# A two-layer graph attention kernel: attention products between two sets of scores, first loads from one queue, and rearranged closing steps

## The chip, the cores and the metric

The kernel runs on one core of a Trainium2 chip. A core has five engines with their own instruction streams: TensorE (PE in the profile) multiplies matrices, VectorE (DVE) and ScalarE (ACT) work element by element, GpSimd (POOL) does too, and SyncE (SP) issues most of the data transfers (DMAs). They wait for each other by semaphores. The metric is the time on the device in microseconds for one execution; the time of a kernel is the median of its runs.

## The reference, cut to what matters

The input is `x`, 128 sequences of 128 rows with 512 features, and `adj`, a mask of 128x128 for each sequence. Two layers follow each other, each with a residual and a layer norm, everything in float32:

```
x = layernorm(x + gnn0(x, adj))     # 4 heads of 64: softmax(where(adj, q k^T / 8, -max)) v, then @ Wo + bo
x = layernorm(x + gnn1(x, adj))     # norm(x)*gamma+beta, 8 heads of 64, mask adj | eye, then @ w_out^T + b_out
```

`gnn0` projects with Wq, Wk, Wv (512 to 256 each) and Wo (256 to 512); `gnn1` has one projection `w_qkv` (512 to 3 x 512) and `w_out` (512 to 512).

## The kernel before, in words

Sequences are handled in 64 groups of two (`G = 2`). The projections are done with a scheme of seven products in place of eight (Strassen's): the two sequences of a group and the two halves of the features are the blocks, `sums` and `weight_sums...` make the added operands, and product numbers 1 to 7 accumulate into the banks `a`, `c` and `f` of PSUM (`INTO`). `product_0` does it for layer 0's projection, `qk` and `v` (through `product`) for layer 1's, `out_product` for both output projections.

The order of the work on every engine is written out by hand (`manual_schedule`): each engine executes in the order in which the program calls it. The main part is `step(s)` for s = 2 to 63, a software pipeline over groups. In step s TensorE does

* the scores of group s - 1 in layer 0 (part 0: both sequences, four heads each) and of group s - 4 in layer 1 (part 1: its first sequence, eight heads; part 2: its second), in `scores`;
* the products of probabilities and values, in `attend`, for group s - 2 in layer 0 (part 0) and s - 5 in layer 1 (parts 1 and 2);
* layer 0's projection of group s, layer 0's output projection of group s - 2, layer 1's projections of group s - 3 and its output projection of group s - 5.

Scores take 64 rows of the array per matmul, two heads side by side; attention products take 64 columns; all the others take the whole array. Between scores and attention products, VectorE puts the scores through the mask into an SBUF tile that POOL has filled with the low value (`masked`, `cleared`), takes row maxima (`maxima`); ScalarE does the exponentials (`exps`); POOL divides by the totals (`normalised`); VectorE turns blocks of 32x32 (`blocks`), and the probabilities are written to DRAM by SyncE and fetched transposed (`put` and `fetch` in `probs_arrive`). Keys and queries of layer 1 take the same kind of way (`kq_arrive`), and ScalarE makes `qo` of them (`q_in_order`, L430). In the first groups and the last ones TensorE transposes instead.

`opening` handles groups 0 and 1 and prepares the weights: `load_transposed` fetches rows of `w_qkv` and `w_out` into buffers that are not in use yet, and `prepare` turns them on TensorE. `closing_a`, `closing_b` (twice) and `last` empty the pipeline: fewer kinds of matmuls are left there to fill the time in which softmax passes through the other engines. `flush` runs norms that were put off; the last group's norm is in `norm_plain`.

PSUM has eight banks: four tiles that rotate (`mm_tile`) and four with fixed names, `a`, `f`, `a0`, `f0`. Layer 1's `v` products use `a` and `f`, as do the attention products of parts 0 and 1; the scores of part 1 use `a0` and `f0`. After products 1, 5 and 6 ScalarE copies the bank (a "tap", L375 and L489) before the next product is accumulated onto it.

In `step`, the stretch around the first part of the change reads:

```python
        made = scores(s)
        ...
        masked(made, s, 0, 1, 2)
        if s == 3:
            turn(s - 3)
            arrive(s - 3)
        attend(s)
        maxima(s, 0, 1)
        out_sums(0, s - 2)
```

Of the kernel before, what the change touches and what calls it, by code (L numbers as in the profile page):

```python
# [17 lines left out]
P = 128  # L18
# [9 lines left out]
def kernel(ctx: ExitStack, tc: tile.TileContext, x, adj, wq, wk, wv, wo, bo,  # L28
# [64 lines left out]
    def load(g):  # L93
        load_rows(g)
        load_mask(g)
# [26 lines left out]


# [3 lines left out]
    nc.vector.tensor_copy(eye, ident)  # L127
# [3 lines left out]

    HF = INNER[0] // 2
    w0 = const.tile([P, KC, 3, 2, HF], F32, name="w0")
    ws0 = const.tile([P, 3, KC // 2, 3, HF], F32, name="ws0")
    for i, w in enumerate((wq, wk, wv)):
        for a in range(4):
            (nc.sync if i else nc.scalar).dma_start(
                w0[32 * a:32 * a + 32, :, i].rearrange("p c h f -> p c (h f)"),
                w[a * P:(a + 1) * P].rearrange("(c i) f -> i c f", i=32))
    load_mask(0)  # L140
    load_rows(0)
    load(1)
    wo0 = const.tile([P, INNER[0] // P, E], F32, name="wo0")
    nc.sync.dma_start(wo0, wo.rearrange("(c p) f -> p c f", p=P))
    bias0 = const.tile([P, E], F32, name="bias0")
    nc.sync.dma_start(bias0, bo[None, :].to_broadcast([P, E]))
    bias1 = const.tile([P, E], F32, name="bias1")
    nc.sync.dma_start(bias1, b_out[None, :].to_broadcast([P, E]))

    transposed(0)  # L150
    load_quarters(1)
# [3 lines left out]
    gb_raw = one.tile([2 * KC, P], F32, tag="sm2", name="gb_raw")  # L155
    gb = const.tile([P, 2 * KC], F32, name="gb")

    setup = []
    def load_transposed(dst, src, name):
        rows, cols = src.shape  # L160
        raws = []
        for r in range(rows // P):
            raw = spare.pop(0)
            nc.sync.dma_start(raw, src[r * P:(r + 1) * P, :])
            raws.append(raw)

        def part(r):
            raw = raws[r]
            pt = mm_tile(f"{name}t_{r}")
            for c in range(cols // P):  # L170
                nc.tensor.transpose(pt[:, c * P:(c + 1) * P], raw[:, c * P:(c + 1) * P], ident)
            to = dst[:, :, r * P:(r + 1) * P]
            pt = pt.rearrange("p (c f) -> p c f", f=P)
            if r % 2:
                nc.scalar.copy(to, pt)
            else:
                nc.vector.tensor_copy(to, pt)

        setup.extend(lambda r=r: part(r) for r in range(rows // P))

    nc.sync.dma_start(gb_raw[:KC], gamma.rearrange("(c p) -> c p", p=P))
# [7 lines left out]


# [23 lines left out]
    def weight_sums_0():  # L214
        combine(*(w0[:, c:c + KH, :, h] for c in (0, KH) for h in range(2)), *(ws0[:, i] for i in range(3)))
# [8 lines left out]

    load_transposed(w1, w_qkv, "w_qkv")
    setup.append(turn_gamma_beta)
    load_transposed(wo1, w_out, "w_out")

    setup.append(setup.pop(-3))
# [71 lines left out]
    def finish_direct(g):  # L301

        xT = XT[1, g] = one.tile([P, KC, T], F32, tag="xT1", name=f"xT1_{g}")
        for b in range(G):
            pt = mm_tile(f"ht{g}_{b}")
            for c in range(KC):
                nc.tensor.transpose(pt[:, c * N:(c + 1) * N], R[g][:, b, c * P:(c + 1) * P], ident)
            for c in range(KC):
                o, i = xT[:, c, b * N:(b + 1) * N], pt[:, c * N:(c + 1) * N]
                scale, bias = gb[:, c:c + 1], gb[:, KC + c:KC + c + 1]  # L310
                if b == 0:
                    nc.scalar.activation(o, i, AF.Identity, bias=bias, scale=scale)
                else:
                    nc.vector.tensor_scalar(o, i, scale, bias, op0=ALU.mult, op1=ALU.add)
        sums(1, g)
# [21 lines left out]
    def product(kind, g, i, take=True):  # L337
# [15 lines left out]
        if first and which == "c":  # L353
            ACC[kind, which] = mm_tile(f"{kind}{which}_{g}")
        elif first:
            ACC[kind, which] = ps_st.tile([P, 512], F32, tag=which, name=f"{kind}{which}_{g}")
# [94 lines left out]
    def product_0(g, *which):  # L451
# [6 lines left out]
        for i in which:  # L458
# [4 lines left out]
            bank, first = INTO[i]  # L463
            if first and bank == "c":
                ACC[0, bank] = mm_tile(f"c0_{g}")
            elif first:
                ACC[0, bank] = ps_st.tile([P, 512], F32, tag=f"{bank}0", name=f"{bank}0_{g}")
            acc = ACC[0, bank]
            parts = acc[:, :3 * P].rearrange("p (t n) -> p t n", n=P)
            if g in PLAIN_0:  # L470
                todo = [(parts[:, (t + odd) % 3], *((right[:, c, t], left[:, c]) if t < 2 else
                                                    (left[:, c], right[:, c, t])))
                        for t in range(3) for c in range(KH)]
# [5 lines left out]
            for n, (o, lhsT, rhs) in enumerate(todo):  # L479
                nc.tensor.matmul(o, lhsT, rhs, start=first and n == 0, stop=n == len(todo) - 1,  # L480
                                 skip_group_check=True)
            src = acc[:, :3 * P]
# [290 lines left out]
    def norm_plain(g, b):  # L773
        row = R[g][:, b]
        n = E // 2
        acc = ACC["op", b]
        st = two.tile([P, 2, nc.vector.BN_STATS_DIM], F32, tag="st_last", name=f"st_last{b}")
        for i in range(2):
            h = slice(i * n, (i + 1) * n)
            nc.vector.tensor_add(row[:, h], acc[:, h], row[:, h])  # L780
            nc.vector.bn_stats(st[:, i], row[:, h])
        mv = two.tile([P, nc.vector.BN_AGGR_DIM], F32, tag="mv", name=f"mv_last{b}")
        nc.vector.bn_aggr(mv, st)
        ve, root = (two.tile([P, 1], F32, tag=t, name=f"{t}_last{b}") for t in ("ve1", "root1"))
        nc.gpsimd.tensor_scalar(ve, mv[:, 1:2], 1.0, EPS, op0=ALU.mult, op1=ALU.add)
        nc.gpsimd.tensor_tensor(root, ve, mhalf[:, :1], op=ALU.pow)
        nc.vector.tensor_scalar(row, row, mv[:, 0:1], root, op0=ALU.subtract, op1=ALU.mult)
        nc.sync.dma_start(out[g * G + b], row)


# [13 lines left out]
    def opening():  # L804
# [4 lines left out]
        for h in range(2):  # L809
            nc.scalar.activation(w0[:, :, 0, h, :], w0[:, :, 0, h, :], AF.Copy, scale=SCALE)  # L810
        product_0(0, 1)
        weight_sums_0()
        product_0(0, 2, 5, 6, 3)
# [31 lines left out]
    def step(s):  # L845

        made = scores(s)
# [6 lines left out]
        masked(made, s, 0, 1, 2)  # L854
        if s == 3:
            turn(s - 3)
            arrive(s - 3)
        attend(s)
        maxima(s, 0, 1)
# [8 lines left out]
        maxima(s, 2)  # L868
# [57 lines left out]
        if s in (3, 4):  # L926
            second = product("v", s - 3, 2, take=False)
            v(s - 3, 1)
            second()
        else:  # L930
            v(s - 3, 1, 2)
# [21 lines left out]
    def closing_a():  # L953
# [31 lines left out]
        blocks(s, 1)  # L985
        exps(s, 2, 1)
# [6 lines left out]
        exps(s, 0, 0)  # L993
        blocks(s, 2)
        probs_arrive(s, 1, 2)
# [8 lines left out]
        cleared(s + 1, 1, 2)  # L1004
# [6 lines left out]
    def closing_b(s):  # L1011

        made = scores(s, 1, 2)
        masked(made, s, 1, 2)
        v(s - 4, 1, 2)
        maxima(s, 1)
        v(s - 4, 6, 5)
        exps(s, 1, 0)
        flush()
        v(s - 4, 7, 3)  # L1020
        maxima(s, 2)
        v(s - 4, 4)
        exps(s, 1, 1)
        normalised(s, 1)
        attend(s, 1, 2)
        out_sums(1, s - 5)
        blocks(s, 1)
        finish_direct(s - 3)
        out_product(1, s - 5, 1, 2)
# [3 lines left out]
        out_product(1, s - 5, 5, 6)  # L1033
        qk(s - 3, 1)
        exps(s, 2, 1)
        out_product(1, s - 5, 7, 3)
        qk(s - 3, 2)
        normalised(s, 2)
        out_product(1, s - 5, 4)
        qk(s - 3, 6)  # L1040
        blocks(s, 2)
        probs_arrive(s, 1, 2)
# [6 lines left out]
        out_product(0, s - 2, 7)  # L1049
        qk(s - 3, 3)  # L1050
        out_product(0, s - 2, 4)
        cleared(s + 1, 1, 2)
# [9 lines left out]
    def last():  # L1062
# [36 lines left out]
        norm_plain(NG - 1, 0)  # L1099
        norm_plain(NG - 1, 1)  # L1100
# [37 lines left out]
```

## Time and profile before

| what | us |
|---|---|
| median of 3 runs | 2755.77 (2754.71 to 2757.05) |
| profiled execution, its own time | 2756.88 |
| span of the profiled execution | 2755.1 |
| TensorE busy | 2725.6 |
| VectorE, POOL, ScalarE busy | 2026.3, 1753.5, 1505.7 |

The profile is of one execution. The span runs from the first instruction to the last; the execution's own time contains 1.8 us more around it. In the lists that follow, a line such as `1312.53 1.16 PE L551 MATMUL sc<-rawqk,qkv ... x16` gives the start in us from the span's start, the length in us, the engine, the line of the kernel, the operation, the tile written and the tiles read, their shapes, and how many records were merged. A float32 matmul leaves two records. A wait is given as who waited, for whom, the sum, how often, and the longest. Matmuls overlap and their ends are modelled, so lengths of work on TensorE are best taken from start to start.

### The profile page before, as it was taken

Reading aid. Unit: us, or ns where it says so; the run is one execution under the profiler, and the core shown is the slowest. Engines: PE = TensorE matmul, PEld = TensorE weight load, DVE = VectorE, ACT = ScalarE, POOL = GpSimd, SP = SyncE. Lnnn points to the kernel's source line nnn. Section 1 sums busy time; section 2 is a strip of 40 time slices with the busy share of each in tenths; the row PEclk is TensorE's granted clock in tenths of the full one; section 3 lists DMA queues with packets and bytes.
Section 4 is the critical chain, followed back from the end, with each engine's and each line's share of the span. In section 5 each row is a group of like instructions: output and inputs, shape, how many; then the busy total and the mean of one; then the engine's idle time right before and its main releaser. Section 6 shows DMA issues by size and latency. Waiting matters only on the chain.

```text
span 2755.1 us, 49293 instructions
## 1 busy us (share of the span) xinstructions
PE 2725.6 (99%) x15781; PEld 2027.5 (74%) x15781; DVE 2026.3 (74%) x3662; ACT 1505.7 (55%) x4805; POOL 1753.5 (64%) x2311
## 2 busy tenths in 40 slices
PE   8999999999999999999999999999999999999998
PEld 7867777677776677776777766777767777667787
DVE  5777777777777777777777777777777777777664
ACT  3455565564564654655645546556556455465554
POOL 4566666666666666666666666666676666666664
PEclk9999999999999999999999999999999999999999
DMA  6567777777777777777777777777777777777741
GB/s 171 154 202 202 222 209 218 210 214 215 215 205 218 218 207 220 212 215 213 211 215 217 202 220 218 204 222 210 214 215 211 220 214 202 220 218 205 212 118 62
DMA packets 548561, 562.72 MB, mean 204 GB/s; under 512 B 55368, under 2 KB 465488, under 8 KB 548304
## 3 DMA queue, kind: packets, MB, share of 16 engines
q1 hardware_dynamic: 547728, 559.05, 71.6%
q8 instruction: 127, 2.08, 0.3%
q14 instruction: 130, 1.06, 0.1%
q10 hardware_dynamic: 576, 0.52, 0.1%
HBM read 300.95 MB, written 258.47 MB: 203 GB/s over the span
## 4 chain that ended last, share of the span: by engine, by line
PE 95%; DMA 2%; POOL 1%; ACT 1%; DVE 1%; issue 0%; SPq 0%; ACTq 0%; POOLq 0%; DVEq 0%
PE qka L365 16%; PE a L480 12%; PE oa L518 11%; PE qkf L365 8%; PE va L365 8%; PE av L680 6%; PE f L480 6%; PE of L518 6%; PE qkc L365 4%; PE vf L365 4%; PE c L480 3%; PE oc L518 3%; PE sc L551 2%; PE sc L557 2%; PE vc L365 2%; PE sc_a L557 2%
## 5 line engine op out<-in xcount | busy, mean ns | idle before, releaser
L601 ACT ACTIVATE sm<-sm,nmax 128x128 f32<-128x128 f32 x1536 | 595.2, 393 | 7.6 <-DVE nmax L592 6.0
L610 POOL TENSOR_TENSOR sm<-sm,rec 128x1024 f32<-128x1024 f32 x192 | 364.3, 1897 | 360.0 <-DVE rec L609 357.9
L702 POOL TENSOR_TENSOR r<-r,bias 128x1024 f32<-128x1024 f32 x128 | 301.7, 2358 | 126.7 <-ACT r L701 126.7
L522 DVE TENSOR_TENSOR r<-oa,r 128x256 f32<-128x256 f32 x508 | 212.0, 417 | 166.3 <-PE oa L518 131.4
L601 ACT ACTIVATION_READ_ACCUMULATOR sm<-sm,nmax 128x1 f32 x1536 | 295.2, 192 | 0.0
L375 ACT COPY ev<-va 128x256 f32<-128x256 f32 x128 | 47.7, 373 | 438.2 <-PE va L365 438.1
L628 DVE STREAM_TRANSPOSE turnedp<-sm 128x1024 f32<-128x1024 f32 x188 | 233.5, 1242 | 65.7 <-POOL sm L610 62.9
L721 POOL TENSOR_SCALAR ve<-mv 128x2 f32<-128x2 f32 x191 | 41.7, 218 | 371.7 <-DVE mv L714 361.1
L747 ACT ACTIVATE r<-r,shift,root 128x512 f32<-128x512 f32 x254 | 192.8, 808 | 85.8 <-POOL shift L736 85.8
L592 DVE TENSOR_REDUCE nmax<-sm 128x8 f32<-128x1024 f32 x192 | 226.1, 1203 | 0.1
L365 PE MATMUL qka<-wsqk,xs 128*128 128x512 f32 x472 | 221.8, 592 | 0.0
L365 PE MATMUL qkf<-w,xs 128*128 128x512 f32 x472 | 221.8, 592 | 0.0
L518 PE MATMUL oa<-wso,so 128*128 128x256 f32 x760 | 206.1, 380 | 2.3 <-POOL so L329 1.8
L518 PE MATMUL of<-wo,so 128*128 128x256 f32 x760 | 206.0, 380 | 0.7 <-POOL so L329 0.4
L329 POOL TENSOR_TENSOR xs<-xT 128x256 f32<-128x256 f32 x256 | 188.6, 737 | 26.8 <-DVE xT L118 23.2
L430 ACT ACTIVATE qo<-kq 128x512 f32<-128x512 f32 x118 | 67.9, 622 | 228.2 <-DMA kq<-scrkq 228.2
L480 PE MATMUL f<-w,xs 128*128 128x128 f32 (+1 forms) x760 | 182.1, 376 | 0.0
L480 PE MATMUL a<-ws,xs 128*128 128x128 f32 (+1 forms) x760 | 182.1, 375 | 0.0
L586 DVE COPY_PREDICATED sm<-m,sc 128x512 f32<-128x512 uint8 x256 | 172.3, 725 | 11.1 <-PE sc L551 2.2
L713 DVE BATCH_NORM_STATS2 st<-r 128x6 f32<-128x512 f32 x254 | 174.8, 688 | 2.3
L572 POOL MEMSET sm<- 128x1024 f32 x192 | 175.2, 954 | 0.0
L365 PEld LDWEIGHTS qkf<-w,xs 128*128 128x128 f32 x472 | 89.7, 190 | 112.9 <-issue 112.9
(179 smaller groups left out, 6506.6 us busy)
## 6 DMA issues: line engine op xcount, KB each, us to landing
scrp<-turnedp SPq DMA_DIRECT2D x188, 512.0 KB, 3.5
pT<-scrp SPq DMA_DIRECT2D x728, 128.0 KB, 2.9
kq<-scrkq SPq DMA_DIRECT2D x236, 256.0 KB, 4.8
x<-in_x_dram SPq DMA_DIRECT2D x256, 128.0 KB, 4.1
r<-in_x_dram SPq DMA_DIRECT2D x64, 512.0 KB, 4.0
out_dram<-r SPq DMA_DIRECT2D x63, 512.0 KB, 3.7
scr<-turned SPq DMA_DIRECT2D x62, 512.0 KB, 6.7
kq<-scr SPq DMA_DIRECT2D x248, 128.0 KB, 2.9
```

The lines of the kernel that those rows point to most:

```text
L329: nc.gpsimd.tensor_tensor(o, a0, a1, op=op)
L365: nc.tensor.matmul(o, lhsT, rhs, start=first and m == 0, stop=m == len(todo) - 1, skip_group_check=True)
L480: nc.tensor.matmul(o, lhsT, rhs, start=first and n == 0, stop=n == len(todo) - 1, skip_group_check=True)
L518: nc.tensor.matmul(acc, left[:, c], right[:, c], start=first and c == 0, stop=c == hk - 1, skip_group_check=True)
L522: nc.vector.tensor_add(part, acc, part)
L572: nc.gpsimd.memset(sm, NEG1 if part else NEG0)
L592: nc.vector.tensor_reduce(NMAX[part], SM[part], AX.X, ALU.max, negate=True)
L601: nc.scalar.activation(sm[:, i, k, :], sm[:, i, k, :], AF.Exp, bias=nmax[:, i, k:k + 1], accum_out=total[:, i, k:k + 1])
L610: nc.gpsimd.tensor_tensor(SM[part], SM[part], rec[:, :, :, None].to_broadcast([P, 2, K1, N]), op=ALU.mult)
L628: nc.vector.transpose(t.rearrange("p q (h r) -> p q h r", r=32), SM.pop(part).rearrange("p i k (q r) -> p q (i k) r", r=32))
L702: nc.gpsimd.tensor_tensor(R[g], R[g], (bias0, bias1)[l][:, None, :].to_broadcast([P, G, E]), op=ALU.add)
L747: nc.scalar.activation(R[g][:, b], R[g][:, b], AF.Identity, bias=shift[:, b:b + 1], scale=root[:, b:b + 1])
```

## The change

In `step`, layer 0's scores (part 0) come first, then the attention products of layer 1's first sequence (part 1), then the scores of parts 1 and 2, and after the masks the other attention products. In step 3 the turn of group 0 goes behind the maxima, and in step 4 the maxima of part 1 go with those of part 2.

The first loads all go through SyncE in the order of use: `x` of group 0, Wk, Wq, Wv, then the first rows of `w_qkv`, group 1's `x`, the first mask, and so on; Wq no longer goes through ScalarE's queue. The copy of the unit matrix `eye` goes from VectorE to ScalarE, the scaling of Wq from ScalarE to VectorE. TensorE does 15 matmuls on the unit matrix, whose result is not used, while the loads are under way. Products 1 and 2 of group 0 and the sums of layer 0's weights are done by projection (`ts`): keys, queries, values.

For groups 0 and 1 the accumulation `va` uses the bank `a0`, and product 2 of `v` follows product 1 in all steps. In `closing_a` one of the fills (`cleared`) comes earlier, and the two parts of the probabilities are fetched separately. In `closing_b` the masks and maxima of part 2, the exponentials, the norms of `flush`, the turns and fetches, and the sums of layer 1's operands change places. In `last` the last norms are split so that the first half of the second sequence is added before the first sequence is written out.

```diff
 # PSUM bank of the first products
-            ACC[kind, which] = ps_st.tile([P, 512], F32, tag=which, name=f"{kind}{which}_{g}")
+            own = kind == "v" and g < 2 and which == "a"
+            ACC[kind, which] = ps_st.tile([P, 512], F32, tag="a0" if own else which, name=f"{kind}{which}_{g}")
 # loads
-    for i, w in enumerate((wq, wk, wv)):
+    for i in (1, 0, 2):
         for a in range(4):
-            (nc.sync if i else nc.scalar).dma_start(
-                w0[32 * a:32 * a + 32, :, i].rearrange("p c h f -> p c (h f)"),
-                w[a * P:(a + 1) * P].rearrange("(c i) f -> i c f", i=32))
-    load_mask(0)
-    load_rows(0)
-    load(1)
...
-    nc.vector.tensor_copy(eye, ident)
+    nc.scalar.copy(eye, ident)
...
+    ready = mm_tile("ready")
+    for _ in range(15):
+        nc.tensor.matmul(ready[:, :P], ident, ident, start=True, stop=True, skip_group_check=True)
...
     transposed(0)
+    load_transposed(w1, w_qkv, "w_qkv", 0, 1, 2, 3)
     load_quarters(1)
+    load_mask(0)
+    load_transposed(w1, w_qkv, "w_qkv", 4, 5)
...
 # opening
-        for h in range(2):
-            nc.scalar.activation(w0[:, :, 0, h, :], w0[:, :, 0, h, :], AF.Copy, scale=SCALE)
-        product_0(0, 1)
-        weight_sums_0()
-        product_0(0, 2, 5, 6, 3)
+        for t in (1, 0, 2):
+            if t == 0:
+                for h in range(2):
+                    nc.vector.tensor_scalar_mul(w0[:, :, 0, h, :], w0[:, :, 0, h, :], SCALE)
+            product_0(0, 1, 2, ts=(t,))
+            weight_sums_0(t)
+        product_0(0, 5, 6, 3)
 # step
-        made = scores(s)
+        made = scores(s, 0)
+        attend(s, 1)
+        made.update(scores(s, 1, 2))
...
         masked(made, s, 0, 1, 2)
+        attend(s, 0, 2)
+        maxima(s, *((0,) if s == 4 else (0, 1)))
         if s == 3:
             turn(s - 3)
             arrive(s - 3)
-        attend(s)
-        maxima(s, 0, 1)
...
-        maxima(s, 2)
+        maxima(s, *((1, 2) if s == 4 else (2,)))
...
-        if s in (3, 4):
-            second = product("v", s - 3, 2, take=False)
-            v(s - 3, 1)
-            second()
-        else:
-            v(s - 3, 1, 2)
+        v(s - 3, 1, 2)
 # closing_a
         blocks(s, 1)
+        cleared(s + 1, 1)
...
+        probs_arrive(s, 1)
         blocks(s, 2)
-        probs_arrive(s, 1, 2)
+        probs_arrive(s, 2)
 # closing_b
-        masked(made, s, 1, 2)
+        masked(made, s, 1)
+        maxima(s, 1)
         v(s - 4, 1, 2)
-        maxima(s, 1)
+        flush()
         v(s - 4, 6, 5)
         exps(s, 1, 0)
-        flush()
         v(s - 4, 7, 3)
-        maxima(s, 2)
+        masked(made, s, 2)
         v(s - 4, 4)
-        exps(s, 1, 1)
-        normalised(s, 1)
         attend(s, 1, 2)
         out_sums(1, s - 5)
-        blocks(s, 1)
+        exps(s, 1, 1)
+        maxima(s, 2)
         finish_direct(s - 3)
+        normalised(s, 1)
...
         out_product(1, s - 5, 5, 6)
+        blocks(s, 1)
+        sums(1, s - 3)
+        exps(s, 2, 1)
         qk(s - 3, 1)
-        exps(s, 2, 1)
+        normalised(s, 2)
         out_product(1, s - 5, 7, 3)
         qk(s - 3, 2)
-        normalised(s, 2)
         out_product(1, s - 5, 4)
+        probs_arrive(s, 1)
+        blocks(s, 2)
+        probs_arrive(s, 2)
+        cleared(s + 1, 1, 2)
         qk(s - 3, 6)
-        blocks(s, 2)
-        probs_arrive(s, 1, 2)
...
 # last
-        norm_plain(NG - 1, 0)
-        norm_plain(NG - 1, 1)
+        for i in range(2):
+            add_plain(NG - 1, 0, i)
+        root = root_plain(0)
+        add_plain(NG - 1, 1, 0)
+        norm_plain(NG - 1, 0, root)
+        add_plain(NG - 1, 1, 1)
+        norm_plain(NG - 1, 1, root_plain(1))
```

`sums(1, g)` no longer stands at the end of `finish_direct`. `add_plain(g, b, i)` adds one half of a row block and takes its statistics, `root_plain` joins them and makes the root on POOL, and `norm_plain` scales and writes out.

## The prediction

> **What bounds the kernel now.** I read the page's busy times first, then who waited on TensorE, then the order of time on TensorE in one ordinary step, in a step with few matmuls and in the first closing step, and last the chain of work near both ends.
>
> ```profile
> PE 2725.6 (99%) x15781; PEld 2027.5 (74%) x15781; DVE 2026.3 (74%) x3662; ACT 1505.7 (55%) x4805; POOL 1753.5 (64%) x2311
> ```
>
> TensorE is busy for 99% of the span: 2755.1 − 2725.6 = 29.5 us are all that it idles. Its waits, in total, times and longest:
>
> ```profile
> PE a L480 <- ACT w L810: 10.2, 1, 10.2
> PE oa L518 <- ACT aT L685: 2.6, 2, 1.6
> PE av L680 <- DMA pT<-scrp: 2.3, 1, 2.3
> PE oa L518 <- POOL so L329: 1.8, 2, 1.1
> PE w_qkvt L171 <- DMA raw_r<-in_L_gnn_w_qkv_dram: 1.5, 1, 1.5
> ```
>
> They occur once or twice, not once per step, so they lie in the opening and the closing. Between 97 and 2600 us TensorE waits for some 2 us in all; a step there takes 42.0 (even) or 42.14 us (odd) and is TensorE's own work. An ordinary step, on the timeline (start, length, engine, line, out<-in):
>
> ```profile
> 1312.53 1.16 PE L551 MATMUL sc<-rawqk,qkv 64*128 64x128 f32 x16
> ...
> 1314.42 1.06 PE L557 MATMUL sc<-kq,qo 64*128 64x128 f32 x16
> 1315.41 1.09 PE L680 MATMUL av<-pT,qkv 128*64 128x128 f32 x16
> 1316.34 1.92 PE L680 MATMUL av<-pT,v 128*64 128x128 f32 x32
> 1318.18 1.13 PE L480 MATMUL a<-w,xT 128*128 128x256 f32 x4
> ```
>
> Ends are modelled, so I go by starts: three score blocks take 1315.41 − 1312.53 = 2.88, three attention blocks 1318.18 − 1315.41 = 2.77. In step 2 there is one block of each:
>
> ```profile
> 61.23 1.16 PE L551 MATMUL sc<-qkv 64*128 64x128 f32 x16
> 62.32 1.09 PE L680 MATMUL av<-pT,qkv 128*64 128x128 f32 x16
> 63.35 1.57 PE L480 MATMUL a<-w,xT 128*128 128x256 f32 x8
> ```
>
> 1.09 and 1.03. So a score block costs (2.88 − 1.09)/2 = 0.895 and a run of them 0.195 once; an attention block 0.87 and a run 0.155 once. A run pays for its change of shape, however many blocks it has. The first closing step has attention followed by scores, the junction that the change adds:
>
> ```profile
> 2620.13 1.09 PE L680 MATMUL av<-pT,qkv 128*64 128x128 f32 x16
> 2621.05 1.92 PE L680 MATMUL av<-pT,v 128*64 128x128 f32 x32
> 2622.90 1.16 PE L551 MATMUL sc<-rawqk,qkv 64*128 64x128 f32 x16
> 2623.99 0.70 PE L518 MATMUL oa<-wo,aT 128*128 128x256 f32 x2
> ```
>
> 2.77 and 1.09 again: the junction is no cheaper there. The chain near the end:
>
> ```profile
> 2707.36 0.69 DVE kq L442
> 2708.24 1.91 POOL sm L610
> 2710.17 1.26 DVE turnedp L628
> 2711.45 3.17 DMA scrp<-turnedp
> ...
> 2717.72 4.58 DMA pT<-scrp
> 2722.39 3.39 PE av L680 x32
> ```
>
> The last probabilities to go through DRAM arrive at 2722.3, while TensorE has been done since 2720.1; the 32 attention matmuls then take 3.3 instead of 1.9.
>
> **What the Trainium skill says.** "TensorEngine Tiling (Array Packing)", Key Properties: changing the tiling mode, not just the tile, drains the engine. Scores use 64 rows, attention 64 columns, the rest 128x128; the 0.155 to 0.195 per run above agree. "TensorE: Matmul & The Clock Gate", Part 1: the clock is halved after idleness and takes a window of sustained work to return. The trace agrees: the first matmuls are 0.213 apart until 15.9 us and 0.112 after, and the granted clock is half from 2722.7 to 2726.1 after the wait above. "DMA: Bandwidth & Descriptors", Queues, rings and completion order: each DMA engine goes round between the queues that have work. The trace agrees: `x` (SyncE's queue) and Wq (ScalarE's), issued together, both have their last part at 8.1 to 8.4 us.
>
> **The change, part by part.**
>
> (1) *`attend(s, 1)` between `scores(s, 0)` and `scores(s, 1, 2)`*, in 59 steps (s = 5 to 63). No matmul is added. Runs go from sc, av to sc, av, sc, av: one score run and one attention run more, 0.195 + 0.155 = 0.35 each step, 59 × 0.35 = **+20.6**. All on the path, since TensorE has no gap to hide it in. Against it: the starts show eleven steps whose score blocks exceed 2.88, by 0.88 (at 216 us), 0.44, 0.34, 0.28 twice and less, 2.8 in all, where the second block waits for `qo` (L430), itself just behind the fetch of `kq`. The moved products give it 1.0 more: **−2.8**. Behind the moved instruction: on TensorE, scores 1 and 2 come 1.0 later, so VectorE's masks end about 0.8 later, and the exponentials start at +7.1 instead of +6.3 into the step. ScalarE regains it: it idles 0.69 before the next tap. The copy of the moved result now stands ahead of ScalarE's two norms (1.5), which end before the copy of `av0` is due. POOL's first `so` ends about 1.4 before `of` needs it. The moved products' own bank is read out (L390) 1.0 before they start, and their probabilities landed long before. SyncE issues the same transfers in the same order, behind the same scores; the puts of parts 0 and 1 go some 0.8 later, and the fetch of `kq`, which follows TensorE's own products, does not move. Cost of these: nothing, range 0 to 0.1 per step, 0 to +6.
>
> (2) *Own bank for `va` of groups 0 and 1*: in steps 3 and 4 the product after `va` starts 1.62 instead of 0.87 later, waiting for its tap, and 0.1 more follows. With `vc` between (0.86) the wait is covered: **−1.7**.
>
> (3) *Opening.* Now Wq and `x` share the DMA engines, ScalarE then loads a table (1.28) and scales Wq (2 × 0.62), and TensorE starts at 10.18, cold. After: sixteen loads of 0.13 MB on one queue, 0.47 each to issue, so issuing ends near 8.3; packets of up to 1 KB moved 0.21 MB per us, so `x`, Wk, Wq, Wv land near 4.9, 7.0, 9.4, 11.9. The eye's copy takes the table load off the path; 15 warm-up matmuls (30 records at 0.213, less once warm) end near 7.3. Keys' products run from 7.1 to 8.0. Wq is scaled on VectorE (two of about 0.55, taken from L787's row) to 10.5, its products to 11.5, values' to 12.9. VectorE's weight sums become three times four of about 0.42; the last set follows Wv and a `qkv` add (0.56), so product 5 ends at 14.65 where it ended at 17.6. The first weight rows come ahead of mask, rows and biases and so no longer stall (1.5); what is pushed back on SyncE's queue still lands in time by the count of bytes (mask 0 near 17 for scores at 22, mask 1 near 31 for 39, rows and bias of group 0 near 25 for POOL's sum after 30). Counting on with the durations of before, the first scores start at 21.9, not 26.76: −4.9. Given back: the bytes are the same and the DMA engines full to 36 us, so group 2's quarters land near 37.5 as now, about when they are needed; +0.5 through the masks of step 2. TensorE idles 2.5 between keys and queries; its clock may fall back, +0.8 (0 to 2). Step 3's turn, with a put and 4 fetches on SyncE behind it, goes behind 1.2 of maxima, whose exponentials so start 1.3 earlier: −0.4; the fetched `kq` comes 1.2 later, and its four scalings end about when the products start. Step 4's maxima for part 1 move behind the sums: ScalarE has other work, nothing. Sum **−4.0**, range −6 to −1.
>
> (4) *Closing steps.* Lost there now, against the rates of the ordinary steps: 0.9 on `va` waiting for VectorE, 1.2 and 1.0 before `oa` and `of` in the first `closing_b`; 1.9, 0.6 and 1.4 in the second; 4.1 at the wait for `pT` (2.5, then the half clock). Walked through in the new order: masks 2 no longer precede the adds; the `aT` copies precede the second four exponentials (1.65), so POOL's sums start 4 earlier; the two last transfers are fetched apart (8 issues of 0.47 instead of 4), and the second turn and its put come before qk 6, so that the fetch lands some 4 us before its products. On POOL a fill (0.92) moves ahead of the second normalisation in `closing_a`, where POOL idles, and `xs` (4 × 0.73) behind the normalisation in `closing_b`; `xs` is due 4 later: nothing. That would save all 11.1; I take **−9.5**, since every gap closed puts the next wait closer. Range −12 to −5.
>
> (5) *Last norms.* The end waits for two adds and two statistics after the last product; one pair (0.42 + 0.43) goes ahead: **−0.8**.
>
> Sum: 20.6 − 2.8 − 1.7 − 4.0 − 9.5 − 0.8 = **+1.8**. The profiled execution took 2756.88, its span 2755.1; so 2758.7 for it. It is 1.1 above the median of 2755.77, so I say 2757.6, rounded to **2758**.
>
> **Rivals.** *The switches are free in the new place* (drains hidden, as the engine already waits for `qo`): then −18.8, 2737. For it: only that the waits of 2.8 exist. Against: the closing step's 1.09 and 2.77. With half the price, 2747. *The closing chain stays the bound*: in `closing_b` the norms now stand on ScalarE ahead of the taps and exponentials; if the turn of the last probabilities still ends within 7 us (put 3.2, fetch 2.2 and more) of its products, the 4.1 at the end stays, and with it some 2 of the earlier gaps: +1.8 + 6 = 2764. It decides once the ends together save under 10.5 of my 14.3. For it: that chain ran through four engines and DRAM; against: the four us of margin. New waits of 0.1 per step would give the same sum. *The change doesn't do what it says*: the matmul order shows the runs split, so only the covered waits could stay uncovered, +2.8.
>
> **How the numbers follow.** A measurement of this kernel tells about 0.2%, 5.5 us. My case 0.50 (2754 to 2762), the closing bound or new waits 0.33 (2761.5 to 2772), cheap switches or larger gains 0.17 (2737 to 2750). Range 2746 to 2770.
>
> **What would show it.** Right: runs of 1.09, 1.02, 1.98, 1.90 in a step of 42.35 and 42.49; first scores near 22; no `pT` wait at the end; a last TensorE stretch that ends earlier. Wrong: an ordinary step still near 42.07, or over 42.6, or closing gaps of over 4 us.

## The result, and the profile after

The changed kernel takes **2761.11 us** in the median (2759.36 to 2762.37), the kernel before 2755.65 beside it (2753.47 to 2758.83): ratio 1.0019, 95% interval 1.0012 to 1.0026. It is slower by 5.5 us; the interval allows 3.3 to 7.2. The profiled execution took 2759.77 and its span is 2758.0, so the two spans differ by 2.9 only: the profiled execution of before was 1.2 above its median, that of after 1.3 below.

The page's busy times and the waits on TensorE of the changed kernel (who, for whom, us in total, times, longest):

```profile
PE 2743.3 (99%) x15811; PEld 2032.5 (74%) x15811; DVE 2033.5 (74%) x3671; ACT 1506.1 (55%) x4804; POOL 1752.0 (64%) x2311
```

```profile
PE a L477 <- DVE w L817: 2.5, 1, 2.5
PE ready L141 <- POOL mhalf L137: 1.3, 1, 1.3
PE of L517 <- DVE r L521: 1.0, 2, 0.8
PE sc_a L556 <- ACT qo L426: 0.9, 1, 0.9
PE qka L361 <- DVE qo L444: 0.4, 1, 0.4
```

The idle time of TensorE has halved (2758.0 − 2743.3 = 14.7 against 29.5), and the large waits of before (10.2 for the weights, 2.6 and 2.3 near the end) are gone. Still the span is longer, so TensorE itself is busier: 17.7 us more, the 30 records of the warm-up (6.1) among them. Where that lies is seen in an ordinary step, on TensorE's timeline (start, length, engine, line, out<-in):

```profile
1315.74 1.16 PE L550 MATMUL sc<-rawqk,qkv 64*128 64x128 f32 x16
1316.83 1.09 PE L679 MATMUL av<-pT,v 128*64 128x128 f32 x16
1317.86 0.37 PE L556 MATMUL sc_a<-kq,qo 64*128 64x128 f32 x1
...
1318.85 1.06 PE L556 MATMUL sc<-kq,qo 64*128 64x128 f32 x16
1319.84 1.09 PE L679 MATMUL av<-pT,qkv 128*64 128x128 f32 x16
```

From start to start the runs take 1.09, 1.03, 1.98 and, to the next `a`, 1.90: 6.00 where two runs took 5.65. The steps take 42.35 and 42.49 where they took 42.00 and 42.14, and not one of the 58 before the last of them shows a wait of over 0.05.

The chain near the end, from SyncE's and TensorE's timelines:

```profile
2714.22 1.73 SPq L242 DMA_DIRECT2D pT<-scrp  x4
...
2719.57 1.73 SPq L242 DMA_DIRECT2D pT<-scrp  x4
...
2725.41 1.13 PE L361 MATMUL va<-w,xT 128*128 128x256 f32 x4
2726.47 1.97 PE L679 MATMUL av<-pT,v 128*64 128x128 f32 x32
```

The last two parts of the probabilities are now fetched apart. The second part is issued from 2719.57 and lands 2.4 to 2.7 after each issue, so by 2723.6, three us before the attention products that wait for it, and these 32 matmuls take 1.90 instead of 3.32, at full clock (before, at half clock). By stretches, each counted from starts on TensorE:

| stretch | before | after | difference | predicted |
|---|---|---|---|---|
| to the scores of step 5 | 132.32 | 127.93 | −4.4 | −5.7 |
| steps 5 to 63 | 2485.75 | 2503.91 | +18.2 | +17.8 |
| closing, to the last projection `op` | 123.37 | 112.06 | −11.3 | −9.5 |
| from the start of `op` to the end | 13.66 | 14.10 | +0.4 | −0.8 |
| sum | | | +2.9 | +1.8 |

### The profile page after: what moved, and what is told of

It is laid out like the page before. It is cut to its first block, busy times and chain, and to the rows that moved or that the text cites. A ratio compares the mean times of both kernels' runs of the same rounds, so it can differ in the third digit from the quotient of the medians.

```text
span 2758.0 us, 49315 instructions
## 1 busy us (share of the span) xinstructions
PE 2743.3 (99%) x15811; PEld 2032.5 (74%) x15811; DVE 2033.5 (74%) x3671; ACT 1506.1 (55%) x4804; POOL 1752.0 (64%) x2311
## 4 chain that ended last, share of the span: by engine, by line
PE 97%; DMA 1%; DVE 1%; issue 0%; SPq 0%; ACT 0%; POOL 0%; POOLq 0%; DVEq 0%; ACTq 0%
PE qka L361 16%; PE a L477 12%; PE oa L517 12%; PE va L361 8%; PE qkf L361 8%; PE av L679 7%; PE f L477 6%; PE of L517 6%; PE vf L361 4%; PE qkc L361 4%; PE oc L517 3%; PE c L477 3%; PE sc L550 2%; PE sc_a L556 2%; PE sc L556 2%; PE vc L361 2%
## 5 line engine op out<-in xcount | busy, mean ns | idle before, releaser
L324 POOL TENSOR_TENSOR so<-aT 128x256 f32<-128x256 f32 (+1 forms) x254 | 150.2, 591 | 52.1 <-ACT aT L682 44.6
L585 DVE COPY_PREDICATED sm<-m,sc 128x512 f32<-128x512 uint8 x256 | 172.4, 727 | 11.1 <-PE sc L550 2.2
```

What stands on the lines that cost most here:

```text
L324: nc.gpsimd.tensor_tensor(o, a0, a1, op=op)
```

## The experiments

Two questions were open: whether the split of the runs, and nothing beside it, makes the steps longer, and by what rule; and what the opening and the end are worth. My theory was that of the prediction, a price per run; its rivals stand with each experiment. Ratios are to the kernel before, run beside it on the same chip. The median of the kernel before was 2755.60, 2757.30 and 2756.38 in the three sets of runs, so kernels of different sets are compared by what each differs from it.

**One part undone.** `e1_joined` is the changed kernel without the split:

```diff
-        made = scores(s, 0)
-        attend(s, 1)
-        made.update(scores(s, 1, 2))
+        made = scores(s)
...
-        attend(s, 0, 2)
+        attend(s)
```

> The changed kernel with one part undone: in each step all three score blocks come first again and all three attention blocks after the masks. Theory (each further run of scores or of attention products costs its change of shape, 0.195 and 0.155, whatever stands before it): 59 x 0.35 = 20.6 less, and the waits for qo that the split had covered, 2.8, come back: 17.8 less than the changed kernel, so about 2743 us, 12.4 under the kernel before (ratio 0.9955); an ordinary step 42.0 and 42.14, with runs of 2.88 and 2.77. Rival (the split is free; the changed kernel lost its gain elsewhere, by waits at its ends): no difference from the changed kernel, 2761 us, ratio 1.002. Second rival (half the price is the split, the rest lies in what follows it): 2752 us.

Measured: 2741.89 us, ratio 0.9951 (0.9938 to 0.9963), 19.2 under the changed kernel, where 17.8 was expected. Steps of 42.00 and 42.14 are back. Counted over steps 5 to 63, whatever exceeds these two lengths sums to 2.6; in the changed kernel what exceeds 42.35 and 42.49 sums to 1.06, of which 0.99 is in the last step alone. The rivals of a free split and of half a price are out.

**That part alone.** `e2_split_only` is the kernel before with the same three lines in place of `scores(s)`.

> The kernel before with one part of the change alone: layer 1's first attention block between the scores of part 0 and those of parts 1 and 2. Theory (price per run): +20.6 for 59 steps, -2.8 for the waits for qo: 2773.5 us, ratio 1.0065; runs of 1.09, 1.02, 1.98 and 1.90 in each step. Rival (the split is free or hidden in the waits): 2753 to 2756 us, ratio 0.999 to 1.000. The four parts add up if this one and the one that undoes it differ from their neighbours by the same amount.

Measured: 2773.27 us, ratio 1.0064 (1.0050 to 1.0078): 17.7 more. The split costs about the same with the old ends as with the new ones. In the two traces steps 5 to 63 grow by 18.0: the 20.6 of the runs, less 2.6 of time beyond the step lengths (3.55 before, 0.93 here). Its five runs lie within 0.44 us (2772.91 to 2773.35), while 25 runs of the kernel before on that chip lie within 4.75. Eight traces with the joined order show 2.6 to 5.3 us beyond the step lengths in these 59 steps, four with a split 0.9 to 1.2. The profile names 0.4 to 2.0 and 0.3 to 1.1 of it as waits, all of them for `qo`.

**The opening alone.** `e4_opening_only` has everything of the change up to the opening's end, the bank of `va` and the moved turn and maxima; steps, closing steps and last norms are those of before.

```diff
+    for i in (1, 0, 2):
...
+            product_0(0, 1, 2, ts=(t,))
+            weight_sums_0(t)
...
+            own = kind == "v" and g < 2 and which == "a"
```

> The kernel before with the opening of the change alone (loads from one queue, copies and scalings moved, warm-up products, products 1 and 2 by projection, own bank of va, the turn and maxima of steps 3 and 4 moved); steps, closing steps and last norms as before. Theory (what the first scores gain, 4.6, is kept but for what steps 2 and 3 give back): TensorE reaches step 5 some 4.4 earlier and keeps it: 2751.3 us, ratio 0.9984. Rival (the transfers, 71% busy in the mean and full in the opening, set the time of step 2; the gain is waited off): 2754 to 2756 us, ratio 0.9995 to 1.000.

Measured: 2752.45 us, ratio 0.9989 (0.9983 to 0.9996): 3.2 less, and runs from 2750.29 to 2755.3. Its profiled execution was one of the faster (2751.33) and had the scores of step 5 at 126.92, 5.4 earlier. So the opening is worth less in the median than in this one execution; why is taken up below.

**The closing steps alone.** `e5_closing_only` is the kernel before with the new `closing_a` and `closing_b`, and `sums(1, s - 3)` in the latter instead of in `finish_direct`.

```diff
-        masked(made, s, 1, 2)
+        masked(made, s, 1)
+        maxima(s, 1)
...
+        probs_arrive(s, 1)
+        blocks(s, 2)
+        probs_arrive(s, 2)
```

> The kernel before with the closing steps of the change alone (the new order in the first closing step and in the two that follow it); opening, steps and last norms as before. Theory (the gaps closed are those of this chain, and depend on nothing before it): from the first scores of the first closing step to the last products 11.3 less, so 2744.4 us, ratio 0.9959; no wait for pT of over 0.3 near the end. Rival (the gaps close only together with the other parts, since the waits for layer 1's queries and for POOL's sums shift with the phase of the transfers): half or less, 2749 us or more.

Measured: 2745.62 us, ratio 0.9966 (0.9954 to 0.9979): 10.0 less (the interval allows 5.8 to 12.7). In its trace, of one of its faster runs (2744.72), the closing stretch takes 111.97, 11.4 less than before. Its waits on TensorE are those of the old opening and nothing for `pT`:

```profile
PE a L479 <- ACT w L809: 10.1, 1, 10.1
PE w_qkvt L171 <- DMA raw_r<-in_L_gnn_w_qkv_dram: 1.3, 1, 1.3
PE va L364 <- ACT ev L374: 1.0, 2, 0.5
...
PE sc_a L556 <- ACT qo L429: 0.4, 2, 0.2
```

The gaps close without the other parts.

**A second dose.** `e3_split_twice` splits each step once more.

```diff
         attend(s, 1)
-        made.update(scores(s, 1, 2))
+        made.update(scores(s, 1))
+        attend(s, 0)
+        made.update(scores(s, 2))
...
-        attend(s, 0, 2)
+        attend(s, 2)
```

> The changed kernel with a second split in each step: scores 0, attention of part 1, scores of part 1, attention of part 0, scores of part 2, attention of part 2, so three runs of each kind instead of two. Theory (each run pays 0.195 or 0.155 once): another 59 x 0.35 = 20.6 and, since no wait for qo is left to cover, nothing against it: 2781.7 us, 26.1 over the kernel before, ratio 1.0095; ordinary steps of 42.70 and 42.84, with score runs of 1.09 and attention runs of 1.03. Rival (the first split pays for a drain that a second one shares): 2761 to 2766 us, ratio 1.002 to 1.004. Second rival (the delayed masks and exponentials, now a further 0.9 later, make TensorE wait too): over 2790 us.

Measured: 2781.7 us, ratio 1.0091 (1.0075 to 1.0106), so 24.4 over the kernel before, where 26.1 was expected; the interval allows both. Steps of 42.70 and 42.84, runs of 1.09 and 1.02: the second split costs 0.35 again, to the hundredth. So far the price per run holds.

**A run apart.** `e6_apart` starts from the joined order and puts one attention block between whole-array products.

```diff
-        attend(s)
+        attend(s, 0, 1)
...
         product_0(s, 1)
+        attend(s, 2)
```

> As the kernel with the split undone (2741.9 us), but layer 1's second attention block stands by itself behind layer 0's first projection product, between matmuls on the whole array. One run of attention more, no run of scores more. Theory (a run pays for itself, 0.155 for attention, whatever its neighbours are): 59 x 0.155 = 9.1 more, 2751 us, ratio 0.9983; the block by itself takes 1.03. Rival (the price belongs to the step between rows and columns of tiles, scores to attention and back; between whole-array matmuls a block is free to stand): no more than the joined order, 2742 us, ratio 0.995.

Measured: 2763.64 us, ratio 1.0024 (1.0015 to 1.0033), 6.3 over the kernel before where the joined order was 13.7 under it, so 20.1 more: both expectations missed. Steps take 42.35 and 42.49, 0.35 more and not 0.155. TensorE's timeline shows where:

```profile
1321.35 1.04 PE L679 MATMUL av<-pT,v 128*64 128x128 f32 x16
1322.32 1.57 PE L477 MATMUL a<-w,xT 128*128 128x256 f32 x8
1323.83 1.09 PE L679 MATMUL av<-pT,v 128*64 128x128 f32 x16
1324.85 0.70 PE L517 MATMUL oa<-wo,aT 128*128 128x256 f32 x2
```

The block apart takes 1.02, which is the 0.155 foreseen. But `a` before it takes 1.51 to the next start, where the same eight records take 1.41 in the joined order, and the two records of `oa` after it 0.54 instead of 0.43. The whole-array products pay at their ends too: breaking them makes one run more of theirs. The layouts so far give one rule:

| order in a step | changes of shape | even and odd step, us | over joined |
|---|---|---|---|
| joined (scores, attention, rest) | 3 | 42.00, 42.14 | |
| split once | 5 | 42.35, 42.49 | 0.35 |
| one block apart | 5 | 42.35, 42.49 | 0.35 |
| split twice | 7 | 42.70, 42.84 | 0.70 |

It is the change of shape that costs. Two more changes cost 0.35, so 0.175 each in the mean, whether they lie between scores and attention or between attention and the whole array. One direction alone was not measured, nor were changes between scores and the whole array added. Another tile of the same shape costs nothing: in the changed kernel products of different tiles on the whole array follow each other at 0.86 to 0.87 (1311.33 to 1314.78). My price per run gave the right sum for the split only since there each new run comes with one change.

**Time for `qo` without a split.** `e9_attention_first` keeps three changes and puts all attention ahead of all scores (with a buffer of its own for `aT` of layer 0).

```diff
+        attend(s, 1, 2, 0)
         made = scores(s)
...
-        attend(s)
```

> As the kernel with the split undone (2741.9 us), but all three attention blocks of a step stand ahead of all three score blocks: one run of each as before, and 2.77 more time for qo. (The copies of layer 0's attention go to a buffer of their own.) Theory (runs are what costs, and the waits for qo, up to 2.8 in the kernel before, come from too little time between the fetch and the scores): steps of 42.0 and 42.14 without exception, 2740 us, ratio 0.994, and runs within 1 us of each other but for the opening. Rival (masks, maxima and exponentials start 2.8 later in every step, and what follows on ScalarE and VectorE comes late for TensorE): a new wait in each step, 0.3 or more, 2758 us or more.

Measured: 2921.6 us, ratio 1.0598 (1.0584 to 1.0613). Its waits on TensorE:

```profile
PE av L679 <- DMA pT<-scrp: 65.9, 58, 2.1
PE oa L517 <- DVE r L521: 19.9, 61, 0.7
PE a L477 <- DVE sm L585: 19.5, 60, 0.3
PE of L517 <- DVE r L521: 12.2, 60, 1.0
```

The theory's steps of 42.0 did not come: they take some 45.1. The four waits sum to 117.5, and the 59 steps take 180 longer than at 42.00 and 42.14, so the profile names only part of the loss. Half of what the rival said is there: VectorE comes late in every step, since its masks start later. The larger wait neither side had: around 1306 and 1351 us the second attention block (`av<-pT,v`, part 2) waits 1.05 and 1.16 for its probabilities. They are the last to be fetched: in the changed kernel, ahead of the step at 1315.74, their four fetches are issued from 1309.54 and take 6.2 to 6.4, so they land from 1315.7 to 1317.4. Part 1's, issued from 1296.28, are in by 1301, so of layer 1's two blocks only part 1's could be moved up.

**The end.** `e12_old_end` is the changed kernel with the last norms in the order of before; `e7_two_banks` is the joined order with the changed end and the last 16 products in two banks.

```diff
 # e12
+        for b in range(2):
+            add_plain(NG - 1, b, 0)
+            add_plain(NG - 1, b, 1)
+            norm_plain(NG - 1, b, root_plain(b))
 # e7
+            ACC["op2", b] = ACC["op", b] if b == 0 else mm_tile("op2")
...
+            acc = ACC[("op", "op2")[i], b]
```

> The changed kernel with the last norms in the order of before: both adds of the first sequence, its norm, then both adds of the second. For the trace. Theory (the second sequence's first add waits for the end of its whole bank, so the first sequence's norm had been free in the wait before it, and the changed order put it between the two adds): 6.49 from the modelled end of the last product to the end of the span, as in the kernel before, instead of 6.92. Rival (the 0.43 are the output transfer's own variation): 6.9.

> The kernel with the split undone (2741.9 us), and the two halves of the last sequence's final products in two banks instead of one. Theory (the changed kernel's first add of the second sequence waited for the end of all 16 products of its bank, and the writing of the first sequence, 0.45, came between that and the second add): the add now comes some 1.3 before the last product ends, so from the end of the last product to the end of the span 5.6 instead of 6.92 us; in all 2740.6 us, which the time alone can't tell from 2741.9, so the trace decides. Rival (the add waits for something else, the last product altogether or POOL's root): the end stays 6.9 us behind the products.

Measured, from the modelled end of the last product to the end of the span: 6.92 in the changed kernel, 6.49 in the kernel before, 6.48 in `e12_old_end` (one run, 2761.15), 5.66 in `e7_two_banks` (2742.7 us, ratio 0.9949, 0.9937 to 0.9962). The other traces agree: 6.9 in all six with the changed end, 6.4 to 6.5 in all five with the old one, 5.7 in all three with two banks. In the times of whole runs these differences drown in the spread. VectorE's timeline in the changed kernel, whose last product ends at 2751.08, and then in `e7_two_banks`, where it ends at 2736.04:

```profile
2751.11 0.42 DVE L779 TENSOR_TENSOR r<-op,r 128x256 f32<-128x256 f32 x1 [1.47 <-PE op L769]
2751.57 0.43 DVE L780 BATCH_NORM_STATS2 st_last<-r 128x6 f32<-128x256 f32 x1
2751.92 0.53 DVE L792 TENSOR_SCALAR r<-r,mv_last,root_last 128x512 f32<-128x512 f32 x1
2752.36 0.42 DVE L779 TENSOR_TENSOR r<-op,r 128x256 f32<-128x256 f32 x1
```

```profile
2734.53 0.37 DVE L780 TENSOR_TENSOR r<-op,r 128x256 f32<-128x256 f32 x1
2734.93 0.43 DVE L781 BATCH_NORM_STATS2 st_last<-r 128x6 f32<-128x256 f32 x1
2735.57 0.55 DVE L793 TENSOR_SCALAR r<-r,mv_last,root_last 128x512 f32<-128x512 f32 x1 [0.21 <-POOL root_last L788]
2736.08 0.42 DVE L780 TENSOR_TENSOR r<-op,r 128x256 f32<-128x256 f32 x1
```

With one bank the first add waits 1.47 for TensorE, until the second half is ready as well; the first sequence's scaling, done in that wait before, then stands between the two adds. With two banks the add runs beside the last products. The Trainium skill ("PSUM — Partial Sum Buffer", Terms) says that TensorE and another engine may not use a bank in the same partitions at the same time; the traces agree, though a program's bookkeeping by tiles, with one tile to a bank here, would look the same, and no run parts the two.

**The opening's pieces.** `e8_no_ready` is the joined order with one warm-up matmul (`range(1)`) instead of 15.

> The kernel with the split undone, and one instead of 15 warm-up matmuls before the first loads have landed. Looked at in the trace, since 1 us is less than the spread of its runs. Theory (the clock is slow until TensorE has worked for some 6 us; the keys' products are then slow inside the 2.5 that the queries wait anyway, but queries and values, 0.9 each at full clock, take twice that): first scores near 23.7 instead of 22.1 where Wk lands at the usual time. Rival (the loads and VectorE's scaling set the time of each group of products, so the slow clock is hidden): first scores no more than 0.3 later.

`e10_turn_back` is `e7_two_banks` with step 3's turn and fetches where they were before:

```diff
+        if s == 3:
+            turn(s - 3)
+            arrive(s - 3)
         attend(s)
         maxima(s, *((0,) if s == 4 else (0, 1)))
-        if s == 3:
-            turn(s - 3)
-            arrive(s - 3)
```

> The kernel with the split undone and the end in two banks, and step 3's turn and fetches of group 0 ahead of the attention products and maxima again, as in the kernel before. For the trace. Theory (the wait of 0.4 to 0.7 for VectorE's qo in step 3, new in the changed kernel, comes from the fetched kq that arrive 1.2 later behind the maxima): the wait is gone and step 3 is 0.4 shorter, 34.05 instead of 34.48. Rival (the wait comes with the weights' sums or with the order of the exponentials): it stays, and the earlier turn costs 0.4 of waits behind the maxima.

`e11_rows_later` is `e10_turn_back` with w_out's loads behind group 2's quarters:

```diff
         load_quarters(2)
+        load_transposed(wo1, w_out, "w_out", 0, 1, 2, 3)
+        setup.append(setup.pop(-3))
```

> As e10_turn_back, and the four loads of w_out's rows (1 MB, needed only near 56 us) issued behind the four quarters of group 2's x instead of ahead of them. Theory (step 2 gives back 1.3 of the 4.6 since these quarters land at 38.5 to 38.7, behind 1 MB that is not needed yet, and VectorE's turn of them stands ahead of the masks): they land some 3 us earlier, step 2 takes 19.25 instead of 20.5, and step 3's scores start near 56.6 to 57 with first scores near 22.1; over all 2740.5 us or a little less, ratio 0.9945, the fastest of these kernels. Rival (what is late in step 2 is the mask or VectorE's own load of work): step 2 stays at 20.5 where it starts near 37.3, 2742 us.

*The turn.* `e10_turn_back` took 2739.15 in its one run. Step 3 takes 34.05, the expected figure, against 34.47 to 34.50 in seven traces with the moved turn. TensorE at the end of the keys' and queries' products of group 0, in the changed kernel and then in this one:

```profile
84.32 2.05 PE L361 MATMUL qka<-xT,wsqk 128*128 128x128 f32 x16 [0.44 <-DVE qo L444]
```

```profile
83.80 1.95 PE L361 MATMUL qka<-xT,wsqk 128*128 128x128 f32 x16
```

The wait is gone, but the theory's cause does not hold. `e8_no_ready` has the moved turn too. ScalarE starts on its fetched `kq` 13.05 after the start of step 3, later than in `e1_joined` (12.05), and yet there is no wait for `qo`: its step 3 takes 33.78, the shortest of all. What parts the traces is on VectorE and POOL just ahead of `qo`, in the changed kernel and then in `e8_no_ready`:

```profile
80.86 2.52 POOL L701 TENSOR_TENSOR r<-r,bias 128x1024 f32<-128x1024 f32 x1
81.09 2.57 DVE L214 TENSOR_TENSOR wsv<-w,wsv 128x256 f32<-128x256 f32 x1
```

```profile
81.92 0.42 DVE L214 TENSOR_TENSOR wsv<-w,wsv 128x256 f32<-128x256 f32 x1
82.52 2.36 POOL L701 TENSOR_TENSOR r<-r,bias 128x1024 f32<-128x1024 f32 x1
```

In the seven traces with the wait, VectorE's last sum of weights begins 0.22 to 0.23 after POOL's addition of the bias, takes 2.57 to 2.58 and ends 0.3 after that addition. In the seven others it is over before POOL begins, and takes 0.42. So the weight sums that the rival named are what holds `qo` up, and with the turn put back they are over before POOL's addition. Why the sum takes so long beside POOL these runs don't show. Something did come back behind the maxima, as the rival also said: at 66.83 `oa` waits 0.44 for `r` (VectorE). `e8_no_ready` waits 0.19 for `r` in this stretch. That the theory's 34.05 came out is luck: against the 34.48 of most traces, `e8_no_ready` is 0.70 shorter without the wait for `qo`, and the old place of the turn is 0.27 longer than that.

*The quarters of group 2.* VectorE's turn of them starts 0.22 after the last of the four has landed; in the changed kernel that is 38.74, with step 2 begun at 37.35:

```profile
38.96 1.30 DVE L118 STREAM_TRANSPOSE xT<-x 128x512 f32<-128x512 f32 x2 [2.56 <-PE sc L550]
40.19 1.32 DVE L585 COPY_PREDICATED sm<-m,sc 128x512 f32<-128x512 uint8 x2
```

The masks stand behind it. In the seven traces in which the last quarter lands over 0.5 after the start of step 2, its landing goes from 37.84 to 40.18, and the scores of step 3 start 19.13 to 19.14 after it in every one: 56.97 in `e4_opening_only`, 57.88 in the changed kernel, 59.31 in `e12_old_end`. Where the landing is early against step 2's start, as in the kernel before (37.82 against 41.99), step 2 takes 19.24 by its own work. In the new opening it takes at least 19.57; where these 0.33 come from I did not follow up. In `e11_rows_later` the quarters land by 34.62, four us earlier, as meant. But that execution began step 2 late, at 38.89, where they no longer decide: step 2 took 19.58, as in `e1_joined` (19.57, begun at 39.04). Its time of 2740.36 us, ratio 0.9943 (0.9930 to 0.9957), is the lowest of the kernels with more than one run, and near the 2740.5 expected, but the runs reach from 2739.34 to 2741.59 and `e10_turn_back` took less in its one run: what this edit takes off step 2 is not shown.

*The clock.* Without the warm-up (`e8_no_ready`, one run, 2742.33) the first scores start at 24.22, half a us later than the theory's 23.7, and the rival is out. With it they start in five traces at 22.03 to 22.38 and in five at 23.26 to 23.81. The windows of TensorE show what parts them (stretch, its length, busy, records, granted clock, DMA share, GB/s), first `e7_two_banks`, then the changed kernel:

```profile
5.60:9.00 3.40, 2.49 (x20) 1.00 1.06 231
9.00:12.40 3.40, 1.24 (x11) 1.00 1.09 264
12.40:15.80 3.40, 3.40 (x19) 0.50 1.12 290
15.80:17.00 1.20, 1.20 (x12) 1.00 1.26 202
```

```profile
6.60:10.00 3.40, 1.94 (x16) 1.00 1.13 235
10.00:13.40 3.40, 2.17 (x19) 1.00 1.07 311
13.40:16.80 3.40, 3.24 (x29) 1.00 1.20 246
```

In both the records are 0.213 apart at first and 0.112 from the first edge on (5.6 and 6.6), and TensorE idles 2.5 near 10. In `e7_two_banks` nearly all of that idle time falls into one window of 3.4, busy for 1.24, and the next window runs at half clock. In the changed kernel, counting on in steps of 3.4 from where the clock rises, an edge lies within it, each window is busy for 1.9 or more, and the clock stays. All ten traces with the warm-up agree: the emptiest such window is busy for 0.95 to 1.42 in the five where the clock falls, and for 1.70 to 2.02 in the five where it stays. The Trainium skill ("TensorE: Matmul & The Clock Gate", Part 1) has the clock judged over windows of 3.4 us that run freely; in `e7_two_banks` the granted clock rises, falls and rises at 5.57, 12.39 and 15.81, 6.82 and 3.41 apart, which agrees. Landing and clock together let the scores of step 5 start anywhere from 126.92 to 129.62 in nine traces with the new opening and its warm-up (the order with attention first left out), against 132.32 to 132.44 in three with the old one: a gain of 2.7 to 5.5, of which the median of `e4_opening_only` (3.2) and its profiled execution (5.4) are two samples.

Against the one trace without it, the warm-up is worth 1.8 to 2.2 where the clock holds and 0.4 to 1.0 where it falls back.

## Why the prediction was right, and where it was off

The kernel became a little slower, as said, since the split costs more than the ends save. The median moved by 5.5 where 1.8 was said.

**The bound and (1), the split: right.** +17.8 was said; +17.7 was measured alone, −19.2 by undoing. Step lengths and runs are those given, to 0.01. The engines behind TensorE cost nothing, as said: the stretch after the attention products takes 36.49 and 36.35 in both kernels. What failed is the rule, which was too narrow (price per change, not per run of scores or attention): it misjudged `e6_apart` by 0.19 a step.

**One new wait was not foreseen.** The first closing step begins with the scores of part 1, so nothing covers `qo` there: 0.99 in the changed kernel, 0.3 to 1.2 in the other split kernels, 0.16 before and none in the other joined ones. Why the split makes this fetch later I did not follow up.

**(2) and (3), bank and opening: mechanism right, sum too large.** Said −5.7; −3.2 in the median. First scores at 21.9 was close (22.13), and `va`'s waits are gone (86.21 and 87.07 start 0.86 apart). The terms that were mis-sized: the quarters of group 2 were put near 37.5 with 0.5 given back, and land at 37.8 to 40.2 with 0.3 to 1.6 given back (step 2 against its 19.24 of before); the moved turn was counted as −0.4, and gives some −0.3 where VectorE's sums run ahead of POOL's addition (33.78 against 34.05), but in seven of the traces they run into it, which was not foreseen, and the turn costs 0.4. The clock, +0.8 (0 to 2) in the sum, is 0 in some executions and 1.1 to 1.7 in others (against 22.13), of which the late landing hides part.

**(4), closing: right.** Said −9.5, with −11.1 by the full walk; −10.0 alone and −11.3 in the profiled pair. The reserve for new waits was not needed: the last fetch lands three us ahead of its products, and the next wait that the prediction feared did not come.

**(5), last norms: wrong in sign.** Said −0.8, measured +0.43. The step that failed is "one pair goes ahead": it took the first half's products for ready before the second's, though both are in one bank.

The parts measured one by one add to 17.7 − 3.2 − 10.0 + 0.4 = +4.9, and +5.5 was measured (3.3 to 7.2); the closing part alone is uncertain by 3 to 4 either way. Against the predicted +1.8, the opening accounts for 2.5 and the end for 1.2.

## What to carry to other kernels

On an engine that is full, count its changes of tile shape in each step, on both sides of a moved block, before counting anything else: two more of them cost more here than all waits that the move removed. Before an operation is split so that half of it goes ahead, see whether both halves wait for the same bank or tile. When a stage starts earlier, list the transfers that it used to find landed: the gain ends at the latest of them. And where a foretold figure comes out, look for a run that has the supposed cause without the effect, as `e8_no_ready` had here.

## What the runs showed of the hardware

* Two more changes of shape on TensorE cost 0.35 us, between 64-row and 64-column matmuls as between 64-column and whole-array ones; four more between 64-row and 64-column cost 0.70.
* A wait of 2.5 us on TensorE drops its clock or not by where it lies against windows of 3.4 us: in ten traces of the same opening, a window busy for 0.95 to 1.42 did, windows busy for 1.70 or more did not. The first scores start 0.9 to 1.8 us later where it drops.
* A sum of 128x256 elements on VectorE took 2.57 instead of 0.42 us when it began just after an addition of 128x1024 on POOL, and TensorE then waited 0.44 to 0.45 for what stood behind it on VectorE (seven traces).
* The order of scores and attention, moved by 2.8 us as a whole, turned a kernel whose TensorE idles for 0.5% of its time (14.7 us in `e1_joined`) into one 6% slower.
